# Layer 1's inverse one product later, and three edits around the first values and the last queries

## The chip, the cores and the metric

The kernel runs on one core of a Trainium2 chip. The metric is device time in microseconds from start to end of the program, as a median of several runs. A run with the hardware profiler gives one execution instruction by instruction; its times are counted from the span's start.

## The reference

Input x has 8 elements of 512 channels by 1024 tokens (32 x 32), fp32. Layer 0 is multi-head attention with 8 heads, layer 1 attention with one head:

```python
# layer 0, per element; x as tokens x channels
xn = layer_norm(x) * gamma + beta            # over channels
q, k, v = (xn @ W.T + b for ...)             # 8 heads of 64
out = softmax(q k^T / 8) v @ Wo.T + bo + x
# layer 1, per element; x as channels x tokens
h = group_norm(x, 32 groups) * gamma + beta
q, k, v = wq h + bq, wk h + bk, wv h + bv
out = x + wp (softmax(q^T k / sqrt(512)) v) + bp
```

## The kernel before

**Products by seven.** Every large matrix product is split into 2 x 2 blocks and computed with seven block products instead of eight, after Strassen and Winograd. `STEPS` lists the seven: which left block or sum (S1 to S4), which right block or difference (T1 to T4), and which of three accumulators x, z, y in PSUM it goes to. The first, second and fourth open x, z and y; the others add onto them. Steps here are counted first to seventh; the code's index is one less. A `Product` is one unit, that is half of the output rows; there are two units to a projection. `multiply` issues a step's matmuls, `tick` pops a number of small jobs (`pieces`) from the deque `side`, and `leave` takes out what the step has completed:

- after the first step ScalarE copies x to a buffer u(0, 0), after the third to u(0, 1), and after the fourth it copies y to u(1, 1);
- after the second VectorE adds z to u(0, 0), after the fifth x to u(1, 1), after the sixth y to u(0, 1) (L386);
- after the seventh ScalarE copies x out as block (1, 0).

So the sixth step, which adds onto y, needs the copy of y done, and the seventh needs the addition of x done. `lead` issues the first half of a step's contraction early.

**Stages of an element.** Layer 0's keys and queries (`project`, from the second element on `project_deep`, which splits the blocks once more and needs "deep" sums of the normed input, L574 to L579), values (`project_v`), the heads' scores and values in pairs, the output projection (`project_out`); then layer 1's group norm (`GroupNorm`), queries, scores (`Whole.scores`), values `vm`, and `Whole.values`, the product of probabilities and values: units `o_units`, accumulators x_o, z_o, y_o, matmuls at L506. All but the last element compute layer 1's queries with `project_mixed`; the last one uses `project` with leads, between the two halves of its group norm.

**Layer 1's inverse.** The softmax's denominators are summed over keys on VectorE and GpSimd, folded by a chain of DMAs into a tile of 128 x 512 (L861, L865), and `Whole.inverse` makes reciprocals of them in three parts: `invert` on VectorE (transpose L869, reduction, reciprocal L1121), `copies` (eight small ScalarE copies, L1455), and `rows` (a VectorE transpose that expands them to rden, L855). The order around it is

```python
            o_units[1].step(2)
            inverse = whole.inverse()
            next(inverse)              # invert
            next(check, None)
            o_units[0].step(1)
            next(inverse)              # copies
            o_units[0].step(1)
            next(inverse)              # rows
```

after which both units' finished blocks are scaled by rden (L1491), have the residual added (L1493, a GpSimd DMA that accumulates) and go out (L1496). Then unit 0 does its fifth to seventh steps and unit 1 its third to seventh, with two ticks each; the deep sums of the next element's normed input are queued after unit 1's third.

**What sets the order.** TensorE, ScalarE, VectorE and GpSimd run in the order in which the program is written (`tc.manual_schedule(engines=ORDERED)`); SP, which issues most loads and stores, is not in that list and is ordered by the framework. Jobs in `side` (the next layer norm's pieces, deep sums, operand differences) fall where ticks fall. A layer norm puts itself back at the second place of `side` after each piece. Semaphores come from the framework, by tiles.

**PSUM.** Three wide tiles of 128 x 1024 (`wide_psum`) and two of 128 x 512 (`bank`). In `banks_of`, y is a bank of its own for each unit; an accumulator named in `own` is a wide tile of its own for each unit (of which 512 columns are used), and any other is one wide tile shared, half and half. The default is `own="x"`.

**Group norm.** `GroupNorm.part` (L1087 to L1117) takes a slice of the chunks: aggregate the statistics, two small products with `grp` in a tile from `self.bank` (pm), the root, and then the normed blocks `gn`, of which some go to ScalarE (L1114) and the others to VectorE (L1116). The last element norms its chunks in two halves, one chunk of each pair at a time, with pm in a wide tile.

Of the kernel before, what the change touches and what calls it, by code (L numbers as in the profile page):

```python
# [71 lines left out]
def fast_path(ctx: ExitStack, tc: tile.TileContext, x: bass.AP, vecs: dict, weights: dict, out: bass.AP,  # L72
# [32 lines left out]
    def big_tile(name):  # L105
        return big.tile([P, S], F32, tag="b", name=name)
# [10 lines left out]
    def block(name):  # L117

        return big_tile(name).rearrange("p (a t) -> p a t", a=2)

    def wide(blk):
        return blk.rearrange("p a t -> p (a t)")
# [56 lines left out]
    ua = const.tile([P, NC], F32, tag="ua", name="ua")  # L179
# [167 lines left out]
    def later(*work):  # L347
        side.extend(work)
# [128 lines left out]
    def channel_part(r):  # L477

        def part(dst, a, b, opens, ks=(0, 1)):
            for k in ks:  # L480
                nc.tensor.matmul(dst, a[:, k, ts(r, P)], b[:, k, :], start=(opens and k == 0), stop=(k == 1),  # L481
                                 skip_group_check=True)
        return part
# [29 lines left out]
    def project(tag, w, bias, h, apart=False, own="x"):  # L513

        res, shared = {}, None if apart else {}

        def unit(r):
            def dest(i, k):
                if (i, k) not in res:
                    res[i, k] = block(f"{tag}_{i}{k}")  # L520
                return res[i, k][:, r, :]

            def shift(u, ps, which, add=None):
                nc.scalar.activation(u, ps, AF.Identity, bias=bias(2 * which[0] + r))

            return Product(f"{tag}_{r}", w, h, channel_part(r), shift, dest,
                           banks_of(tag, r, shared, own))
        return [unit(r) for r in range(2)], res
# [287 lines left out]
    def project_v(tag, w, h, apart=False):  # L816


        res, shared = {}, None if apart else {}

        def unit(r):
            def dest(i, k):
                if (i, k) not in res:
                    res[i, k] = big_tile(f"{tag}_{i}{k}")
                return res[i, k][:, ts(r, HB)]

            return Product(f"{tag}_{r}", w, h, token_part(r), plain_shift, dest, banks_of(tag, r, shared))
        return [unit(r) for r in range(2)], res
# [6 lines left out]
    def operands(h):  # L835

        return {"tag": h["tag"], **{f"{j + 1}{k + 1}": h[j, k] for j in range(2) for k in range(2) if (j, k) in h}}

    def add_operand(b, n):
        b[n] = block(f"{n}_{b['tag']}")  # L840
        l, r = {"T1": ("12", "11"), "T2": ("22", "T1"), "T3": ("22", "12"), "T4": ("21", "T2")}[n]
        nc.vector.tensor_sub(wide(b[n]), wide(b[l]), wide(b[r]))

    def add_operands(b):
        later(*(lambda n=n: add_operand(b, n) for n in ("T1", "T2", "T3", "T4") if n not in b))


    def compact(t, ps):
# [213 lines left out]
    class GroupNorm:  # L1062
# [10 lines left out]
        def part(self, chunks):  # L1073

            own = list(range(NC // 2))[chunks]
            n = 2 * len(own)
            name = f"{self.b}_{own[0]}"

            def of(t):
                return t.rearrange("p (j a) -> p a j", j=2)[:, chunks, :]  # L1080

            def wide_of(t):
                return t[:, :n].rearrange("p (a j) -> p a j", j=2)

            for a in own:
                for j in range(2):
                    c = 2 * j + a  # L1087
                    nc.vector.bn_aggr(self.mv[:, c, :], self.stats[:, c, :, :].rearrange("p a s -> p (a s)"))
            mu, var = (of(self.mv[:, :, i]) for i in range(2))
            mean, dev, sc, sh = (of(t) for t in (self.mean, self.dev, self.sc, self.sh))  # L1090
            yield
            ps = self.bank(f"pm_{name}")
            pm = wide_of(ps)
            nc.tensor.matmul(pm, grp, mu, start=True, stop=True)
            nc.vector.tensor_copy(mean, pm)
            nc.vector.tensor_sub(dev, mu, mean)
            nc.vector.tensor_mul(dev, dev, dev)
            nc.vector.tensor_add(dev, dev, var)
            yield
            pv = wide_of(ps[:, 2 * NC :])  # L1100
            nc.tensor.matmul(pv, grp, dev, start=True, stop=True)
            inverse_root(sc, pv, "gsc")()
            nc.vector.tensor_mul(sc, sc, of(vt[:, VECS.index("g1"), :]))
            nc.vector.tensor_mul(sh, mean, sc)
            nc.vector.tensor_sub(sh, of(vt[:, VECS.index("be1"), :]), sh)
            for j, k in ((0, 0), (1, 0), (0, 1), (1, 1)):
                if (j, k) not in self.h:
                    self.h[j, k] = block(f"gn_{self.b}_{j}{k}")
                for a in own:
                    c = 2 * j + a  # L1110
                    m, d = self.sc[:, c : c + 1], self.sh[:, c : c + 1]
                    h, x = self.h[j, k][:, a, :], self.xt[j, k][:, a, :]
                    if a == own[0] and k == 0:
                        nc.scalar.activation(h, x, AF.Identity, bias=d, scale=m)  # L1114
                    else:
                        nc.vector.tensor_scalar(h, x, m, d, ALU.mult, ALU.add)  # L1116
            yield  # L1117
# [426 lines left out]
    def bias_of(n):  # L1544
        return lambda oc: vec(n, oc)

    with tc.manual_schedule(engines=ORDERED):
# [51 lines left out]
        units, kt = project("k0", wk_now, bias_of("bk0"), hb)  # L1599
# [5 lines left out]
        units, qt = project("q0", wq_now, bias_of("bq0"), hb)  # L1605
# [7 lines left out]
        save_deep_later("q", wq_now)  # L1613
        save_deep_later("a", wa, (1, 2))
        units, vts = project_v("v0", wv_now, hb)
        for u in units:
            u.pieces = 2
            u.rest()
        for b in range(B):
            more = b + 1 < B  # L1620
# [43 lines left out]
            o_units, x1 = project_out(b, wo_now, ob, stats)  # L1664
# [8 lines left out]
            wa_now = load_w("a", b)  # L1673
            if more:
                wa_deep = load_deep("a", b, (1, 2))
            gn = GroupNorm(b, x1, stats)
# [27 lines left out]
            h1b = operands(h1)  # L1704
# [3 lines left out]
            if more:  # L1708
                def vn_put_away():
                    for ik, t in vn.items():  # L1710
                        vn_away[ik] = put_away(t, f"v_away_{b + 1}_{ik[0]}{ik[1]}")
                    if ln:
                        ln.sums()

                vn_away = {}
                spare = list(x1)
                whole = Whole(b, {}, h1b, x1_away)

                def ready(t):
                    whole.q["11"] = t  # L1720
                    whole.query_prime("11")

                qa, closing = project_mixed(f"qa{b}", wa_now, wa_deep, lambda oc: ua[:, oc : oc + 1], h1b, primes,
                                            lambda: n_units[1].step(1), vn_put_away,
                                            lambda: residual(*spare.pop(0)), ready)
                whole.q["12"] = qa[1, 0]
                whole.deep_query("12")
                closing(whole.q)
            else:
                a_units, qa = project(f"qa{b}", wa_now, lambda oc: ua[:, oc : oc + 1], h1b, own="")  # L1730
                h1b["T1"] = t1
                leads = [(u, i) for i in (0, 1, 3) for u in a_units]
                until(lambda: not side)
                for n, _ in enumerate(gn.part(slice(1, 2))):
                    for u, i in ((leads[:3], leads[3:4], leads[4:])[n]):
                        u.lead(i)
                nc.vector.tensor_sub(t1[:, 1, :], h1[0, 1][:, 1, :], h1[0, 0][:, 1, :])
                add_operands(h1b)
                a_units[0].step(2)
                a_units[1].step(2)  # L1740
                away = list(x1)
                for n, (_, name) in enumerate(SINGLES):
                    deep_operands_later(h1b, h1_deep, [name])
                    later(*(lambda ik=ik: residual(*ik) for ik in away[n : n + 1]))
                for u in a_units:
                    u.pieces = 2
                a_units[0].rest()
                whole = Whole(b, qa, h1b, x1_away)
                whole.deep_query("11")
                a_units[1].step(5)  # L1750
                whole.deep_query("12")
# [16 lines left out]
            o_units = whole.values(vm)  # L1768
# [7 lines left out]
                ln.queue()  # L1776
            o_units[1].step(2)
            inverse = whole.inverse()
            next(inverse)
            next(check, None)  # L1780
            o_units[0].step(1)
            next(inverse)
            o_units[0].step(1)
            next(inverse)
            for u in o_units:
                u.hold = False
# [413 lines left out]
```

## Time and profile before

| | |
|---|---|
| median of 3 runs | 2809.73 us (2807.9 to 2809.82) |
| the profiled execution | 2808.93 us; its span 2807.1 us |
| TensorE busy | 2789.8 us of the span (99%) |
| VectorE, ScalarE, GpSimd busy | 2095.0, 1248.4, 527.6 us |
| granted TensorE clock | 0.999 |
| first x_o to first x_k, element 0 to 6 | 49.07, 49.35, 48.34, 49.86, 48.35, 49.50, 48.06 us |

A timeline line gives start and duration in us, engine, line of the program, operation, output and inputs with shapes, and the number of instructions merged; a bracket gives the idle time before it and what ended it. A line of the waits gives the total in us, how often, and the longest.

### The profile page before, as it was taken

The numbers are of one execution on the slowest core, as the hardware profiler recorded it, in microseconds if no ns is written. First come the engines' busy times: TensorE is split into PE (matmuls) and PEld (weight loads), VectorE is DVE, ScalarE is ACT, GpSimd is POOL, SyncE is SP. The second block draws the span as 40 slices with busy tenths as digits, with TensorE's granted clock in tenths as the row PEclk, the third lists the DMA queues.
The fourth block names the chain that finished last, engine by engine and source line by source line (L and its number), as shares of the span: only waits on it lengthen the run. The fifth ranks groups of instructions, "written<-read, shape, count | busy, mean of one in ns | idle before, by whom it ended". The sixth has DMA issues, their size and how long they took to land.

```text
span 2807.1 us, 31693 instructions
## 1 busy us (share of the span) xinstructions
PE 2789.8 (99%) x10959; PEld 1624.5 (58%) x10959; DVE 2095.0 (75%) x2978; ACT 1248.4 (44%) x2114; POOL 527.6 (19%) x724
## 2 busy tenths in 40 slices
PE   9999999999999999999999999999999999999999
PEld 4535756358563685536854467644676347663375
DVE  6677877778777777777867777678867778657775
ACT  4463425724257242662436533365334733336341
POOL 2031022210222102220122211222112210122001
PEclk9999999999999999999999999999999999999999
DMA  8245367353763547536474464744448433373224
GB/s 314 95 96 126 109 163 189 69 149 111 170 160 70 166 107 184 126 78 190 108 177 109 88 186 107 200 79 119 149 112 207 100 94 117 82 195 64 65 79 99
DMA packets 141018, 365.56 MB, mean 130 GB/s; under 512 B 19776, under 2 KB 24176, under 8 KB 140848
## 3 DMA queue, kind: packets, MB, share of 16 engines
q0 software_dynamic: 58992, 144.22, 27.7%
q1 hardware_dynamic: 81760, 219.19, 22.6%
q8 instruction: 89, 1.46, 0.2%
q14 instruction: 81, 0.66, 0.1%
q10 hardware_dynamic: 96, 0.02, 0.0%
HBM read 198.21 MB, written 63.44 MB: 93 GB/s over the span
## 4 chain that ended last, share of the span: by engine, by line
PE 93%; DMA 3%; DVE 2%; issue 1%; POOL 0%; ACT 0%; SPq 0%; POOLq 0%; DVEq 0%; ACTq 0%
PE s L1154 16%; PE acc L1172 16%; PE s L1320 7%; PE x_o L506 6%; PE x_v L490 4%; PE x_out L481 4%; PE x_vm L490 3%; PE y_s L1320 3%; PE y_o L506 3%; PE y_v L490 2%; PE s L1355 2%; PE y_out L481 2%; PE x_k L604 2%; PE x_q L604 2%; PE c_qa L698 2%; PE y_vm L490 1%
## 5 line engine op out<-in xcount | busy, mean ns | idle before, releaser
L1163 DVE TENSOR_TENSOR sum<-sum,p 128x1024 f32<-128x1024 f32 x384 | 470.3, 1225 | 39.4 <-DVE sum L1161 0.5
L1157 ACT ACTIVATE p<-s 128x1024 f32<-128x1024 f32 (+1 forms) x608 | 478.8, 984 | 15.1 <-PE s L1154 15.1
L1172 PE MATMUL acc<-p,v_again 128*64 128x512 f32 x1792 | 390.9, 594 | 0.0
L1172 PEld LDWEIGHTS acc<-p,v_again 128*64 128x64 f32 x1792 | 126.1, 137 | 261.3 <-issue 236.7
L861 POOL DMA_DIRECT2D fold<-sum x312 | 207.7, 759 | 302.8 <-DMA sum<-sum 176.7
L1154 PE MATMUL s<-q,k 64*128 64x512 f32 x1152 | 252.1, 592 | 0.0
L1154 PE MATMUL s<-q_lower,k_lower 64*128 64x512 f32 x896 | 196.1, 592 | 0.0
L1161 DVE TENSOR_TENSOR sum<-p,p 128x1024 f32<-128x1024 f32 x64 | 78.2, 1221 | 154.5 <-ACT p L1157 154.5
L1154 PEld LDWEIGHTS s<-q,k 64*128 64x128 f32 x1152 | 109.7, 186 | 138.2 <-issue 84.9
L865 POOL DMA_DIRECT2D sum<-sum x78 | 63.5, 814 | 456.6 <-DVE sum L1163 232.5
L1154 PEld LDWEIGHTS s<-q_lower,k_lower 64*128 64x128 f32 x896 | 85.4, 186 | 110.5 <-issue 68.5
L1176 ACT COPY o<-acc 128x512 f32<-128x512 f32 x63 | 36.9, 586 | 221.7 <-PE acc L1172 221.5
L1360 DVE TENSOR_TENSOR p<-p,p 128x1024 f32<-128x1024 f32 x96 | 114.0, 1214 | 6.3 <-ACT p L511 6.3
L506 PE MATMUL x_o<-T_p,S_vm 128*128 128x512 f32 x256 | 115.2, 592 | 0.0
L511 ACT COPY u(0, 0)_v<-x_v 128x512 f32<-128x512 f32 x16 | 9.4, 586 | 186.5 <-PE x_v L490 186.5
L1416 POOL DMA_DIRECT2D sum<-p x32 | 28.0, 934 | 334.2 <-ACT p L1308 240.8
L490 PE MATMUL x_vm<-w_m,T_gn 128*128 128x256 f32 x384 | 90.7, 379 | 0.0
L481 PE MATMUL x_out<-T_o,w_o 128*128 128x512 f32 x192 | 89.2, 594 | 0.0
L506 PEld LDWEIGHTS x_o<-T_p,S_vm 128*128 128x128 f32 x256 | 48.6, 190 | 60.7 <-issue 60.7
L1218 ACT COPY rr<-r 32x16 f32<-32x16 f32 x256 | 53.5, 209 | 62.0 <-DVE r L1121 58.6
L490 PE MATMUL x_v<-w_v,T_h 128*128 128x256 f32 x336 | 80.0, 381 | 0.0
L490 PEld LDWEIGHTS x_vm<-w_m,T_gn 128*128 128x128 f32 x384 | 72.9, 190 | 10.0
(621 smaller groups left out, 5456.1 us busy)
## 6 DMA issues: line engine op xcount, KB each, us to landing
sum<-sum POOLq DMA_DIRECT2D x78, 256.0 KB, 3.4
fold<-sum POOLq DMA_DIRECT2D x312, 64.0 KB, 2.3
x<-in_x_dram SPq DMA_DIRECT2D x32, 512.0 KB, 4.7
xr<-in_x_dram SPq DMA_DIRECT2D x64, 256.0 KB, 4.9
x_away<-x SPq DMA_DIRECT2D x32, 512.0 KB, 3.3
sum<-p POOLq DMA_DIRECT2D x32, 512.0 KB, 5.9
v_away<-v SPq DMA_DIRECT2D x28, 512.0 KB
v_again<-v_away SPq DMA_DIRECT2D x28, 512.0 KB, 7.3
```

Of the source, the lines that this page charges most:

```text
L481: nc.tensor.matmul(dst, a[:, k, ts(r, P)], b[:, k, :], start=(opens and k == 0), stop=(k == 1), skip_group_check=True)
L490: nc.tensor.matmul(dst[:, ts(m, CB)], b[:, k, ts(2 * r + m, P)], a[:, k, :], start=(opens and m == 0 and k == 0), stop=(k == 1), skip_grou ...
L506: nc.tensor.matmul(dst, a[:, m, ts(r, P)], b[m // 2][:, m % 2, :], start=(opens and m == 0), stop=(m == NM // 2 - 1), skip_group_check=True)
L604: nc.tensor.matmul(dst[:, ts(s, CB)], a[s], b[s], start=(opens and s == 0), stop=True, skip_group_check=True)
L861: nc.gpsimd.dma_start(out=f[ts(q + i, BL), :], in_=t[ts(n, BL), ts(i, HB)], accum_op=ALU.add if n else ALU.bypass)
L1154: nc.tensor.matmul(parts[i], self.k[m // 4][r, ts(m % 4, P)], self.q[r, :], start=True, stop=True)
L1157: nc.scalar.activation(dst, src, AF.Exp, scale=1.0 / float(D) ** 0.5)
L1161: nc.vector.tensor_add(self.sum, self.p[0], p)
L1163: nc.vector.tensor_add(self.sum, self.sum, p)
L1172: nc.tensor.matmul(acc[i * D : (i + 1) * D, :], value_of(self.vt, m, self.c * P + i * D, D), self.p[m][:, ts(i, HB)], start=(m == 0), stop ...
L1320: nc.tensor.matmul(dst[:, ts(c, CB)], x[0][:, ts(c, P)], a[0], start=(opens and c == 0), stop=True, skip_group_check=True)
L1360: nc.vector.tensor_add(wide(t), wide(t), wide(x))
```

## The change

Four edits, and one that lets a queued operand be made earlier:

- In all elements but the last, unit 0's third step comes ahead of `invert`, its fourth ahead of `copies`, and unit 1's third ahead of `rows`. Unit 1's third step thus comes before unit 0's fifth, with one tick in place of two.
- In the last element's queries each unit has an x tile of its own, all three wide tiles are opened ahead of the second half of the group norm, and that half's pm is a bank.
- There, T2 is queued first and an empty job after it, so that T3 is made two ticks later than before, behind unit 0's first addition. `add_operands` skips what is there already.
- In a group norm of one chunk (the last element's halves) ScalarE takes the second token half instead of the first, and VectorE the first. With two chunks nothing changes.
- In the first element's values, unit 0's first step has no tick.

```diff
     def add_operands(b):
-        later(*(lambda n=n: add_operand(b, n) for n in ("T1", "T2", "T3", "T4") if n not in b))
+        later(*(lambda n=n: n in b or add_operand(b, n) for n in ("T1", "T2", "T3", "T4") if n not in b))
...
-                    if a == own[0] and k == 0:
+                    if a == own[0] and k == len(own) % 2:
...
         units, vts = project_v("v0", wv_now, hb)
+        units[0].pieces = 0
+        units[0].step(1)
         for u in units:
...
-                a_units, qa = project(f"qa{b}", wa_now, lambda oc: ua[:, oc : oc + 1], h1b, own="")
+                a_units, qa = project(f"qa{b}", wa_now, lambda oc: ua[:, oc : oc + 1], h1b)
+                for u, to in ((0, "x"), (0, "z"), (1, "x")):
+                    a_units[u].open(to, True)
+                gn.bank = bank
...
                 nc.vector.tensor_sub(t1[:, 1, :], h1[0, 1][:, 1, :], h1[0, 0][:, 1, :])
+                later(lambda: add_operand(h1b, "T2"), nothing)
                 add_operands(h1b)
...
             inverse = whole.inverse()
+            if more:
+                o_units[0].step(1)
             next(inverse)
             next(check, None)
             o_units[0].step(1)
             next(inverse)
-            o_units[0].step(1)
+            o_units[0 if not more else 1].step(1)
             next(inverse)
```

## The prediction

> **What bounds the kernel now.** I read the page's head first, then TensorE's waits, then the timeline around each wait.
>
> ```profile
> span 2807.1 us, 31693 instructions
> ...
> PE 2789.8 (99%) x10959; PEld 1624.5 (58%) x10959; DVE 2095.0 (75%) x2978; ACT 1248.4 (44%) x2114; POOL 527.6 (19%) x724
> ...
> PE 93%; DMA 3%; DVE 2%; issue 1%; POOL 0%; ACT 0%; SPq 0%; POOLq 0%; DVEq 0%; ACTq 0%
> ```
>
> TensorE is idle for 17.3 of 2807.1 us, and the change takes no matmul away. So the whole stake is a part of those 17.3 us, and what matters is which holes the edits reach. The list of waits on TensorE names them (total, times, longest):
>
> ```profile
> PE y_o L506 <- ACT u(1, 1)_o L511: 1.9, 3, 0.9
> PE x_o L506 <- DVE u(1, 1)_o L386: 1.3, 4, 0.3
> PE x_qa L481 <- ACT gn L1114: 0.8, 1, 0.8
> PE x_qa L481 <- ACT qa L524: 0.8, 1, 0.8
> PE z_qa L481 <- DVE qa L386: 0.8, 1, 0.8
> PE x_v L490 <- ACT u(0, 0)_v L511: 0.4, 1, 0.4
> ```
>
> The rest is the start of the kernel and its tail, which the change doesn't touch. A wait costs more than its entry, since the refill behind it is not in the list; so I measure holes by start times. The timeline of element 3 (the fourth) shows the repeated one, TensorE first, then ScalarE, then VectorE:
>
> ```profile
> 1420.41 3.60 PE L506 MATMUL x_o<-T_p,S_vm 128*128 128x512 f32 x8
> 1424.94 3.70 PE L506 MATMUL y_o<-p,S_vm 128*128 128x512 f32 x8 [0.93 <-ACT u(1, 1)_o L511]
> 1428.96 3.70 PE L506 MATMUL x_o<-T_p,vm 128*128 128x512 f32 x8 [0.32 <-DVE u(1, 1)_o L386]
> ...
> 1422.58 1.70 ACT L1455 COPY rr<-r 32x16 f32<-32x16 f32 x8 [4.76 <-DVE r L1121]
> 1424.30 0.59 ACT L511 COPY u(1, 1)_o<-y_o 128x512 f32<-128x512 f32 x1
> ...
> 1420.06 0.71 DVE L869 STREAM_TRANSPOSE fold1t<-fold 128x512 f32<-128x512 f32 x1 [5.55 <-DMA fold<-sum]
> 1428.26 0.65 DVE L386 TENSOR_TENSOR u(1, 1)_o<-u(1, 1)_o,x_o 128x512 f32<-128x512 f32 x1
> ```
>
> The folded sums land late, VectorE inverts them late, ScalarE's eight small copies of the inverse wait for that, and the copy that frees bank y (its product ended near 1420.4) stands behind them in the queue. Unit 0's sixth product needs that bank; its seventh then waits for VectorE's sum, which is behind the inverse as well.
>
> [...] the 0.59 us copy starts only at 1424.30, when the small copies end. [...] The trace does show such waits (x_qa at 2676.84 below): this program waits by tile, so a tile per unit removes them. [...]
>
> **Layer 1's inverse, elements 0 to 6.** A product of a unit is 8 records at 0.429 us, 3.433 us by start times. From the first x_o to the first x_k there are 14, which is 48.06 us. Element 6 takes 48.06 (2426.57 to 2474.63). The others take 49.07, 49.35, 48.34, 49.86, 48.35, 49.50. Their losses are 1.01 + 1.29 + 0.28 + 1.80 + 0.29 + 1.44 = **6.11 us**. Element 6 has no layer norm to prepare, and its fold lands early.
>
> The edit moves unit 0's third product ahead of the inversion, the fourth ahead of the small copies, and unit 1's third ahead of the row expansion. Let F be the time from the start of unit 0's third product to VectorE's fold transpose: 5.73, 6.00, 5.00, 6.51, 5.02, 6.17 us in elements 0 to 5. It ends a chain of GpSimd's DMAs that no moved instruction feeds, so I keep it.
> - Bank y: product four ends 6.9 us after that start. Its copy is now ahead of the small copies and is done by 7.7; the sixth product starts at 4 x 3.433 = 13.7. This wait goes.
> - The sum before the seventh product. VectorE from F: inversion 2.52, small copies on ScalarE 1.74, rden 1.26, two scalings 1.22, expansion of mu 1.16. One tick more has gone by, so a centring (L967, 1.17) now stands there too, and the mean's folding (2.15) has moved ahead of the inversion, into VectorE's wait. Then the sum, 0.65. That is F + 9.7 = 16.2 at worst, against 5 x 3.433 = 17.17. Cover left: 0.9 us in element 3, 2.4 in elements 2 and 4.
> - What is late next: unit 1's third product is no longer followed by two ticks. The deep operands of the next keys therefore start one product later and have one piece fewer behind them at the hand-over. In element 3, K is x_k's start, 1449.67. VectorE's last scaling starts at K + 0.81 in both. Before, three pieces followed until 22_deep was complete at 1453.48 = K + 3.81; now 21's first piece (L574, 0.70) joins them: K + 4.51. x_k reads it at 1454.41 = K + 4.74. With 0.05 for the semaphore (sum ends 1428.91, TensorE starts 1428.96) **0.2 us** of cover is left. If it is gone, each 0.1 late costs 0.1 plus a refill of 0.1, six times over.
> - Queues moved past: GpSimd's additions (L1493) and SP's output stores follow the scalings, which stay at F + 6.8 in elements 0 to 5. In element 6 they come one product, 3.4 us, later; SP's w_k_deep loads behind them were issued by 2457.1 and take 7.5 us to land, so they arrive by 2468 for an x_k at 2474.6. The next layer norm's x landed tens of us before (issued by 1383 for a use at 1429).
>
> I take the full 6.11. If the seventh product still waits and 22_deep is late, some 0.3 each, it is 6.11 - 6 x 0.6 = 2.5. It can't exceed 6.11.
>
> **First element's values.** z_v starts at 99.55 and y_v at 103.69: 4.14 us for two products of 1.727, **0.69 us** lost. Unit 0's first copy stands behind a squaring (100.28 to 101.33) which a tick put there. Without that tick it follows q's copy (99.70 to 100.28) and ends near 100.9, ahead of the 101.28 at which x_v can start. The squaring moves into the next tick. Bounds 0 and 0.69; I take 0.69. No instruction is added; two pieces pass to the pairs' ticks.
>
> **Last element's queries.**
>
> ```profile
> 2663.16 1.12 PE L481 MATMUL x_qa<-gn,w_a 128*128 128x512 f32 x2 [0.78 <-ACT gn L1114]
> 2666.94 1.12 PE L481 MATMUL z_qa<-gn,w_a 128*128 128x512 f32 x2 [0.76 <-DVE qa L386]
> ...
> 2674.18 1.88 PE L481 MATMUL x_qa<-T_gn,w_a 128*128 128x512 f32 x4
> 2676.84 1.98 PE L481 MATMUL x_qa<-T_gn,w_a 128*128 128x512 f32 x4 [0.78 <-ACT qa L524]
> ```
>
> - First normed block: VectorE writes one in 0.54 (L1116), ScalarE in 0.82 here. x_qa can start at 2662.29 + 0.54 + 0.05 = 2662.88 instead of 2663.16.
> - T1's second half (2663.21) and T2 (2663.93, next start 2665.07) stay; T2's other operand, now from ScalarE, is ready at 2663.81. Without T3 in between, the sum that reads z runs from 2665.07 to 2665.75, not 2666.21 to 2666.89. z is still one tile, so unit 1's z starts at 2665.80 instead of 2666.94: **1.14 us**, the 0.28 within it. T3 then ends at 2666.9, for a use at 2669.4.
> - The x tile: unit 1's third product follows unit 0's seventh at once, 1.72 instead of 2.66 us later: **0.94 us**.
> - Given back: a residual's pair of activations (1.3 us) falls between two of unit 1's copies, as it does in unit 0 now: 0.03 to 0.1. The statistics' products move to a bank, since three tiles hold all the wide space. The last lead, y_qa of unit 1, gets that bank after VectorE's read at 2661.28, where it would start anyway (2661.27), and has until 2662.88.
>
> Sum **2.05 us**. Bounds: 0.9 (the x tile alone) and 2.9 (the list's three waits with their refills, of which the first can't vanish wholly).
>
> **Sum.** 6.11 + 0.69 + 2.05 = 8.85 us. The profiled execution took 2808.93 us (span 2807.1, the rest around it): 2800.1. The median of the runs is 0.8 above it, so 2809.73 - 8.85 = **2800.9 us**.
>
> **Rivals.**
> 1. *Part of it is eaten*: the 0.2 us at 22_deep or the 0.9 us ahead of the seventh product doesn't hold. For it: both covers are small and F moves by 1.5 us between elements. Against: each is worked from rows of the same stretch. Gain 4 to 7, about 2804.
> 2. *The change doesn't do what it says*: F grows, since GpSimd's fold transfers drift and meet others, or SP's free order puts another wait in; the holes reappear a product later. Against: F is at most 6.5 and would have to reach some 10 for bank y's user to wait as now. Gain 0 to 3, about 2808.
> 3. *Slower*: the next keys' weights come late. SP's order isn't written out, and its w_k and w_k_deep loads stand behind stores that wait for the scalings. If x_k then waits in all seven elements, it decides for slower by 0.2% from (5.6 + 8.85) / 7 = 2.1 us each; at 2.5 us it is 2800.9 + 17.5 = 2818. For it: stores and loads share a queue. Against: landing by about 1442.6 for 1449.7 in element 3, 7 us before its use, 5 after the gain; no wait on a DMA is listed for TensorE in any element's body.
>
> **How the numbers follow.** About 0.2% (5.6 us) is what a measurement of this kernel can tell from no change. As worked out (2799.3 to 2803, scatter of the runs included): 0.70. Rival 1: 0.15, half of it beyond 5.6. Rival 2: 0.07. Rival 3: 0.08. Faster 0.70 + 0.07 = 0.77, same 0.08 + 0.07 = 0.15, slower 0.08. The range is 2799.3 (the bounds' 9.7 us, less likely in full, and a 0.7 us lower run) to 2805.8, which takes in most of rival 1: about 0.8.
>
> **What would show it.** Right: no y_o or x_o wait at L506; ScalarE's u(1, 1)_o copy ahead of the eight L1455 copies; 48.1 us from the first x_o to the first x_k in every element; in the first values z_v to y_v 3.45; in the last element, z_qa near 1.1 earlier against the first x_qa lead, and no x_qa wait on qa. Wrong: an x_k wait on 22_deep (L578 or L579), an x_o wait on VectorE in element 3, or any TensorE wait on w_k.

## The result, and the profile after

| | before | after |
|---|---|---|
| median of 7 runs each | 2809.73 us (2807.9 to 2810.03) | 2800.16 us (2798.97 to 2800.33) |
| span of the profiled execution | 2807.1 us | 2797.2 us |
| first x_o to first x_k, elements 0 to 6 | 49.07, 49.35, 48.34, 49.86, 48.35, 49.50, 48.06 us | 48.06 to 48.07 us in all |
| F (third step's start to the fold transpose), elements 0 to 5 | 5.73, 6.00, 5.00, 6.51, 5.02, 6.17 us | 5.82, 7.10, 4.69, 6.66, 4.64, 6.28 us |
| first values, z_v to y_v | 4.14 us | 3.46 us |
| last element, first x_qa lead to the first score | 28.37 us | 26.34 us |

The ratio of the times is 0.9967, with a 95% interval of 0.9955 to 0.9979. Here are the head of the changed kernel's page, with busy time, share and count, and its chain that ended last:

```profile
span 2797.2 us, 31704 instructions
...
PE 2786.4 (100%) x10959; PEld 1625.5 (58%) x10959; DVE 2095.1 (75%) x2978; ACT 1248.2 (45%) x2114; POOL 527.6 (19%) x724
...
PE 99%; DMA 0%; DVE 0%; ACT 0%; issue 0%; SPq 0%; DVEq 0%
```

The matmuls are as many as before, and the other engines are as busy as before. TensorE's idle time fell from 17.3 to 10.8 us, and the chain that ended last now stays on TensorE almost throughout. These are TensorE's longest waits in the changed kernel (total, times, longest):

```profile
PE pst_k L301 <- DMA w_k<-in_L_conv_wk_dram: 1.8, 1, 1.8
PE ps_first L1550 <- DVE checks L142: 1.3, 1, 1.3
PE pm L1094 <- DVE mv L1088: 0.6, 1, 0.6
PE x_qa L481 <- DVE gn L1116: 0.4, 1, 0.4
```

Of the six waits that the prediction showed, one is still in this list: x_qa's on the normed block, cut from 0.8 to 0.4 us. Of z_qa's wait on the sum, 0.14 us are left in the trace, too little for the list. The first two lines belong to the start of the kernel (both end before 20 us), and the third was there before, with the same 0.6 us. The same stretch of element 3 in the changed kernel's timeline, TensorE first, then ScalarE, then VectorE:

```profile
1416.36 7.03 PE L506 MATMUL x_o<-T_p,S_vm 128*128 128x512 f32 x16
1423.22 3.60 PE L506 MATMUL y_o<-p,S_vm 128*128 128x512 f32 x8
1426.66 3.60 PE L506 MATMUL x_o<-T_p,vm 128*128 128x512 f32 x8
...
1416.61 0.58 ACT L511 COPY u(1, 1)_o<-y_o 128x512 f32<-128x512 f32 x1 [2.85 <-PE y_o L506]
1418.67 1.70 ACT L1455 COPY rr<-r 32x16 f32<-32x16 f32 x8 [1.47 <-DVE r L1121]
...
1416.15 0.71 DVE L869 STREAM_TRANSPOSE fold1t<-fold 128x512 f32<-128x512 f32 x1 [3.75 <-DMA fold<-sum]
1424.16 1.23 DVE L967 TENSOR_TENSOR x<-x,mu 128x1024 f32<-128x1024 f32 x1
1425.30 0.68 DVE L386 TENSOR_TENSOR u(1, 1)_o<-u(1, 1)_o,x_o 128x512 f32<-128x512 f32 x1
```

The copy of y now stands ahead of the eight small copies and waits for nothing but its own product. VectorE still waits 3.75 us for the fold, and the fold is as late as before: F is 6.66 us here, and was 6.51. But TensorE has one more product to do meanwhile: the 16 records at 1416.36 are unit 1's third and unit 0's fifth. The sum ends at 1425.98, 0.68 us ahead of the seventh product.

The last element's timeline in the changed kernel, TensorE only:

```profile
2655.33 1.12 PE L481 MATMUL x_qa<-gn,w_a 128*128 128x512 f32 x2 [0.43 <-DVE gn L1116]
...
2658.31 1.13 PE L481 MATMUL z_qa<-gn,w_a 128*128 128x512 f32 x2
...
2665.55 3.60 PE L481 MATMUL x_qa<-T_gn,w_a 128*128 128x512 f32 x8
```

Unit 1's z product starts 2.98 us after the x_qa, where it was 3.78, and both units' third products run as one group of eight records, where the second had to wait.

The spans differ by 9.9 us: 6.1 in the inverses, 0.7 in the first values and 2.0 in the last queries, which is 8.8. Another 0.8 lies ahead of the first x_v, in code that the change doesn't touch: x_v starts at 97.82 us before and at 97.01 after, and it lies between 97.0 and 98.4 in all profiles of this study. The remaining 0.3 is in the tail with its output transfers.

### The profile page after: what moved, and what is told of

It is laid out like the page before. It is cut to its first block, busy times and chain, and to the rows that moved or that the text cites. A ratio compares the mean times of both kernels' runs of the same rounds, so it can differ in the third digit from the quotient of the medians.

```text
span 2797.2 us, 31704 instructions
## 1 busy us (share of the span) xinstructions
PE 2786.4 (100%) x10959; PEld 1625.5 (58%) x10959; DVE 2095.1 (75%) x2978; ACT 1248.2 (45%) x2114; POOL 527.6 (19%) x724
## 4 chain that ended last, share of the span: by engine, by line
PE 99%; DMA 0%; DVE 0%; ACT 0%; issue 0%; SPq 0%; DVEq 0%
PE s L1154 16%; PE acc L1172 16%; PE x_o L506 8%; PE s L1320 7%; PE x_v L490 4%; PE x_vm L490 4%; PE y_o L506 4%; PE x_out L481 4%; PE y_s L1320 3%; PE y_v L490 2%; PE y_vm L490 2%; PE s L1355 2%; PE y_out L481 2%; PE z_o L506 2%; PE x_q L604 2%; PE x_k L604 2%
## 5 line engine op out<-in xcount | busy, mean ns | idle before, releaser
L506 PE MATMUL x_o<-T_p,S_vm 128*128 128x512 f32 x256 | 114.0, 592 | 0.0
L506 PEld LDWEIGHTS x_o<-T_p,S_vm 128*128 128x128 f32 x256 | 48.6, 190 | 60.7 <-issue 60.5
```

What stands on the lines that cost most here:

```text
L506: nc.tensor.matmul(dst, a[:, m, ts(r, P)], b[m // 2][:, m % 2, :], start=(opens and m == 0), stop=(m == NM // 2 - 1), skip_group_check=True)
```

## The experiments

My theory was that ScalarE's queue behind the late fold makes the holes of the inverse, that one more product on TensorE covers it, and that the waits by tile and the order of VectorE's sums make those of the last queries. The rivals were that only part of a gain is kept, that the holes come back later, and that the cover at 22_deep is nearly used up.

### One part at a time

The kernel before with the inverse's edit alone:

```diff
             inverse = whole.inverse()
+            if more:
+                o_units[0].step(1)
             next(inverse)
             next(check, None)
             o_units[0].step(1)
             next(inverse)
-            o_units[0].step(1)
+            o_units[0 if not more else 1].step(1)
             next(inverse)
```

> The inverse's edit alone. Theory (the queue order on ScalarE and VectorE made the holes): first x_o to first x_k is 48.06 in all seven elements, no TensorE wait at L506, 6.1 us below the kernel before (ratio 0.9978). Rival (the gain of the whole change is mostly elsewhere, or the start of the kernel): less than 4 us.

Measured: 2802.43 us against 2809.2 for the kernel before on the same chip, ratio 0.9976 (0.9967 to 0.9985), so 6.8 us. All elements take 48.06 to 48.07 us, and the last queries stay at 28.39. The inverse's edit acts alone and in full.

The kernel before with the last element's edits alone:

```diff
-        later(*(lambda n=n: add_operand(b, n) for n in ("T1", "T2", "T3", "T4") if n not in b))
+        later(*(lambda n=n: n in b or add_operand(b, n) for n in ("T1", "T2", "T3", "T4") if n not in b))
...
-                    if a == own[0] and k == 0:
+                    if a == own[0] and k == len(own) % 2:
...
-                a_units, qa = project(f"qa{b}", wa_now, lambda oc: ua[:, oc : oc + 1], h1b, own="")
+                a_units, qa = project(f"qa{b}", wa_now, lambda oc: ua[:, oc : oc + 1], h1b)
+                for u, to in ((0, "x"), (0, "z"), (1, "x")):
+                    a_units[u].open(to, True)
+                gn.bank = bank
...
+                later(lambda: add_operand(h1b, "T2"), nothing)
                 add_operands(h1b)
```

> The last element's three edits alone (a tile x for each unit, T3 later, first normed block on VectorE). Theory: from the first x_qa lead to the first score 26.3 us instead of 28.37, so 2.05 us below before; the elements keep their L506 waits (losses of some 6 us). Rival: below 1 us, since a later stage takes it back.

Measured: 2807.4 us, ratio 0.9993 (0.9984 to 1.0001). The time alone can't tell this from no change. The trace can: the lead-to-score stretch takes 26.35 us instead of 28.37. It also shows something about the inverse, whose order is here that of the kernel before: its elements lose 7.06 us in this execution, where they lost 6.1 in the one that I had worked from. The fold came 6.83 us after the third product in element 1, instead of 6.00, which is most of the difference.

The kernel before with the first values' edit alone:

```diff
         units, vts = project_v("v0", wv_now, hb)
+        units[0].pieces = 0
+        units[0].step(1)
         for u in units:
```

> The missing tick in the first element's values alone. Theory: z_v to y_v 3.46 us instead of 4.14; 0.7 us in all, less than a measurement tells. Rival: the squaring that moves into the next tick delays a later copy, and the 0.7 come back before the first score s.

Measured: 2809.02 us, ratio 0.9998 (0.999 to 1.0007). z_v to y_v takes 3.45 us instead of 4.14, and from x_v to the first score it is 25.47 instead of 26.16, so the 0.69 us aren't given back there. The inverse's losses are 7.19 us in this execution. The three medians together differ from before by 6.8 + 1.8 + 0.2 = 8.8 us, against 9.6 for the whole change; with the intervals above, that is the same.

### Is the late fold the root?

The kernel before, in its old order, with the halving ahead of layer 1's fold left out. This leaves part of the sum out of the denominators (half of the rows that should be added), and with it transfers of the chain on which VectorE waits:

```diff
         def fold(self):
             self.f = half_tile(f"fold1_{self.b}")
-            for hf in range(NH):
-                halve(self.total[hf])
             for hf in range(NH):
                 fold(self.f, 2 * hf, self.total[hf])
```

> The kernel before with layer 1's fold made shorter: the DMA additions of the upper 64 rows (halve) are left out there, so layer 1's denominators miss half of their rows; all else is as before. Theory (the holes come from the late fold, which the queues pass on): VectorE's fold transpose comes some 3 us after unit 0's third product instead of 5 to 6.5, and all seven elements take 48.06 with the order unchanged: 6.1 us below before. Rival (the order itself costs, whenever the fold lands): the holes of 0.3 to 1.8 us stay.

Measured: 2802.58 us, ratio 0.9976 (0.9966 to 0.9986), with 48.06 to 48.07 us in every element although no product was moved. F is 0.9 to 2.0 us; I had expected some 3. The fold's tile in this kernel, with VectorE's idle time ahead of it and how often:

```profile
  DMA fold<-sum: 2.9, 4
```

The kernel before has 28.9 us in 7 such waits. So the fold's lateness is the root, and moving products (6.8 us) gains what an early fold gains (6.6).

### Would ScalarE's order have been enough?

The kernel before with the small copies put behind unit 0's fourth product, and unit 1's third left where it was:

```diff
             inverse = whole.inverse()
+            if more:
+                o_units[0].step(1)
             next(inverse)
             next(check, None)
             o_units[0].step(1)
             next(inverse)
-            o_units[0].step(1)
+            if not more:
+                o_units[0].step(1)
             next(inverse)
```

> The kernel before with one thing moved: unit 0's fourth product ahead of the small copies; unit 1's third product stays where it was, and the inversion stays ahead of unit 0's third. Bank y's copy is then ahead of the small copies. Theory: no y_o wait, but the sum ahead of the seventh product ends at about F + 8.5 against 13.7, so x_o waits of about 0.5, 0.8, 0, 1.3, 0 and 1.0 us with their refills in elements 0 to 5: some 4 of the 6.11 us stay. Rival (the queue order on ScalarE is all there is): every element takes 48.06.

Measured: 2811.81 us in a single run, beside 2809.7. The elements take 48.92, 49.93, 48.20, 51.91, 48.13, 49.98 and 48.06 us, a loss of 8.7, where I had expected about 4. The wait for bank y is gone; TensorE's waits in this kernel name what stands in its place:

```profile
PE x_o L506 <- DVE u(1, 1)_o L386: 5.7, 4, 1.9
```

Without unit 1's product in between, the seventh comes 4 x 3.433 = 13.7 us after the third, but VectorE's sum ends F + 8.85 after it, 15.7 in element 3. I had put it at F + 8.5, since I forgot the mean's folding (2.15 us at L869 to L940, where I had counted 1.74 for the small copies), which here, as in the kernel before, stands between the inversion and rden.

So the order on ScalarE gains nothing by itself, and the comparison with the kernel before says more than that: the wait for bank y never set the loss. Four profiles have the whole fold and lack the additional product: before, the last queries alone, the first values alone, and this one. In each of their elements 0 to 5 the loss is F - 4.73 us to within 0.02, with y's copy behind the small copies or ahead of them; elements 3 and 4 of this kernel are the exceptions. (In element 4, F - 4.73 is below zero and 0.06 us are lost; on element 3 see below.) VectorE takes 8.85 us from the fold transpose to the end of the sum in all of them (9.00 in that element 4), as in element 3 here:

```profile
1421.09 0.71 DVE L869 STREAM_TRANSPOSE fold1t<-fold 128x512 f32<-128x512 f32 x1 [5.91 <-DMA fold<-sum]
1429.29 0.65 DVE L386 TENSOR_TENSOR u(1, 1)_o<-u(1, 1)_o,x_o 128x512 f32<-128x512 f32 x1
```

The seventh product starts 0.05 us after that sum. In the kernel before, the sixth product's wait for bank y was a part of the same hole, taken one product early. What gains is the 3.4 us of work that TensorE does in the meantime. Whether y's copy has to be moved at all was not run. In the three profiles with the old order it ends F + 4.83 us after the third product starts, 11.3 in element 3 before; with one product more the sixth would start at 13.7, so by this estimate the additional product alone would have covered that wait as well.

In element 3, 1.70 us more were lost than F - 4.73. Its timeline, TensorE only:

```profile
1429.99 5.40 PE L506 MATMUL x_o<-T_p,vm 128*128 128x512 f32 x8 [1.88 <-DVE u(1, 1)_o L386]
1435.23 3.60 PE L506 MATMUL x_o<-T_p,S_vm 128*128 128x512 f32 x8
```

The eight records behind the hole take 5.24 us by start times, not 3.43. Stretches of the same kernel, two in element 3 and, beside them, one with the gap of element 5, say why (length; busy us of TensorE, weight load, VectorE, ScalarE and GpSimd, each with its count; granted clock; DMA share; GB/s):

```profile
1427.47:1430.89 3.42, 1.54 (x4) 0.49 (x3) 3.39 (x6) 0.00 (x0) 1.82 (x2) 1.00 0.41 48
1430.89:1434.30 3.41, 3.41 (x5) 1.35 (x4) 3.38 (x5) 2.11 (x2) 0.87 (x1) 0.50 0.96 159
...
2113.55:2116.96 3.41, 1.76 (x5) 0.66 (x4) 3.38 (x5) 0.00 (x0) 1.82 (x2) 1.00 0.44 65
```

The granted clock is 0.50 for 3.41 us behind the hole, which is 1.7 us of time. TensorE's gap between products was 2.0 us here (5.47 from start to start of two products of 3.43), and the half clock began 0.9 us after its end. Elements 1 and 5 had gaps of 1.8 us of the same kind, and no slower products behind them (3.54 and 3.53 us by start times, with 0.1 of refill). In the stretch ahead of the half clock TensorE was busy for 1.54 of 3.42 us, and in that of element 5, at a clock of 1.00, for 1.76 of 3.41. What sets the one gap apart from the other two was not shown.

### The last element, edit by edit

From here on the base is the kernel after. First, both units share one x tile again, and the second half's statistics are back in a wide tile:

```diff
-                a_units, qa = project(f"qa{b}", wa_now, lambda oc: ua[:, oc : oc + 1], h1b)
-                for u, to in ((0, "x"), (0, "z"), (1, "x")):
-                    a_units[u].open(to, True)
-                gn.bank = bank
+                a_units, qa = project(f"qa{b}", wa_now, lambda oc: ua[:, oc : oc + 1], h1b, own="")
```

> The changed kernel with the x tile shared again by both units of the last queries (and the statistics in a wide tile). Theory: the 0.94 us wait of unit 1's third product on the copy of qa is back, so first lead to first score 27.3 us instead of 26.34. Rival (the tile is not what is waited for): 26.3.

Measured: 2801.21 us in a single run; lead to score takes 27.39 us, 1.05 more than after. In its timeline the wait of unit 1's third product is back, 0.94 us by start times, to which 0.1 us of refill comes (the four records behind the wait take 1.99 us, the four ahead of it 1.88):

```profile
2669.34 1.99 PE L481 MATMUL x_qa<-T_gn,w_a 128*128 128x512 f32 x4 [0.78 <-ACT qa L524]
```

Next, T3 made at its old place, ahead of the first addition:

```diff
-                later(lambda: add_operand(h1b, "T2"), nothing)
```

> The changed kernel with T3 queued at once again. Theory: unit 1's z waits for the sum behind T3, 1.14 us later, so first lead to first score 27.5 us. Rival: the x tile already took this wait, 26.3.

Measured: 2802.42 us in a single run; lead to score takes 27.48 us, 1.14 more than after. Unit 1's z product waits:

```profile
2660.86 1.12 PE L481 MATMUL z_qa<-gn,w_a 128*128 128x512 f32 x2 [1.28 <-DVE qa L386]
```

Third, the first normed block written by ScalarE again:

```diff
-                    if a == own[0] and k == len(own) % 2:
+                    if a == own[0] and k == 0:
```

> The changed kernel with the first normed block on ScalarE again. Theory: x_qa starts 0.28 us later, but unit 1's z is set by VectorE's T1, T2 and sum, so first lead to first score stays within 0.05 of 26.34: this edit is hidden by the wait behind it. Rival: 26.6, the 0.28 is on the path.

Measured: 2801.56 us in a single run; lead to score takes 26.46 us, 0.12 more than after. The wait is 0.27 us longer than after's 0.43:

```profile
2657.06 1.13 PE L481 MATMUL x_qa<-gn,w_a 128*128 128x512 f32 x2 [0.70 <-ACT gn L1114]
```

Of the 0.27 us at this place, 0.15 are made up at unit 1's z, which then waits less; 0.12 are kept. I had expected it to be hidden almost wholly.

### How much cover is left at 22_deep?

The kernel after, with one product more of unit 1 issued ahead of the queuing of the deep sums:

```diff
-            o_units[1].step(1)
+            o_units[1].step(2 if more else 1)
```

> The changed kernel with the next keys' deep sums queued behind unit 1's fifth product instead of its fourth, so two pieces more are left at the hand-over. Theory (0.2 us of cover in the changed kernel): the deep sum of 22 is complete at about x_k's start + 5.3 against a need at 4.7, so x_k waits 0.6 us with a refill of 0.1 in elements 0 to 5, 4 us in all over the changed kernel; element 6, which has no layer norm between, doesn't wait. If only the slice that is read counts, some 0.2 each and 1 us in all. Rival (cover is larger than worked out): no wait.

Measured: 2809.26 us, ratio to before 0.9999 (0.999 to 1.0007), so nearly the whole gain is lost. The stretch from the first x_k to the first x_q takes 22.93 us instead of 21.56 in each of the elements 0 to 5, and is unchanged in element 6. Six times 1.37 is 8.2 us, twice what I had expected; a wait of 0.7 us for a w_q_deep load comes once beside it. In element 3 of this kernel, TensorE, then VectorE:

```profile
1456.69 0.70 PE L604 MATMUL x_k<-22_deep_h,w_k_deep 128*128 128x256 f32 x2 [1.10 <-DVE 22_deep_h L578]
...
1455.02 1.28 DVE L386 TENSOR_TENSOR k<-u(0, 0)_k,z_k 128x512 f32<-128x512 f32 x2
1456.21 0.42 DVE L578 TENSOR_TENSOR 22_deep_h<-22_deep_h,x 128x256 f32<-128x256 f32 x1
1456.67 0.43 DVE L579 TENSOR_TENSOR 22_deep_h<-x,22_deep_h 128x256 f32<-128x256 f32 x1
```

Two things are to be seen here. First, 22_deep's last piece has fallen behind two additions of k (1.19 us from their start to that of L578), because they are issued before the deep sums are emptied from the queue; I had left them out, and they make the wait larger than I thought. Second, x_k starts at 1456.69, 0.06 us after L578 ends (1456.63) and well before L579 ends (1457.10). It needs only the part that L578 writes. So the waits of this program aren't by whole tiles everywhere, as I had put it above: here the instruction that writes the slice counted, while x_qa's wait on the other unit's half (0.78 us, gone with a tile for each unit) went by the tile. So in the kernel after, where L578 ends at K + 4.09 with x_k due at K + 4.74, the cover is 0.6 us, not the 0.2 that I had worked out from L579.

### What is still to be had

The kernel after, with unit 1's z product later, so that it no longer waits for the sum that reads z:

```diff
                 a_units[0].step(2)
-                a_units[1].step(2)
+                a_units[1].step(1)
+                a_units[0].step(1)
+                a_units[1].step(1)
```

> The changed kernel with unit 0's third product of the last queries put between unit 1's first and second. Theory: unit 1's z no longer waits for the sum (0.3 us with the refill), first lead to first score 25.95 to 26.05 instead of 26.34. Rival: T2 is not ready in time and the wait only moves, 26.3.

Measured: 2799.62 us in a single run; lead to score takes 25.75 us, 0.59 less than after, where I had expected 0.29 to 0.39. The z product now follows its neighbours without a gap; gaps of less than 0.1 us between the products behind it are gone as well.

The same, and in addition one more product of the output projection ahead of the first statistics of the group norm:

```diff
-                for _ in gn.part(slice(0, 1)):
-                    o_units[1].step(1)
+                for n, _ in enumerate(gn.part(slice(0, 1))):
+                    o_units[1].step(2 if n == 0 else 1)
...
-                a_units[1].step(2)
+                a_units[1].step(1)
+                a_units[0].step(1)
+                a_units[1].step(1)
```

> The last one's edit, and unit 1's fourth output product put ahead of the first statistics product of the last group norm. Theory: the wait of pm (0.56 us) goes, but the first half's norm comes 1.2 us later and pushes VectorE's chain to the second half's statistics, so x_qa's wait grows by 0.4 to 0.9 and little is won over the last kernel: within 0.5 us of it. Rival: VectorE has room, 0.6 us less.

Measured: 2799.01 us (2798.86 to 2800.41), ratio to before 0.9963 (0.9949 to 0.9977). The first half's wait at pm is gone, but the second half's product with the statistics now waits, as TensorE's timeline of this kernel shows:

```profile
2652.00 0.38 PE L1094 MATMUL pm<-mv,grp 128*128 128x2 f32 x2 [0.31 <-DVE mv L1088]
```

I had expected it at x_qa, whose wait stays as it was (0.44). From the first x_out to the first score it takes 51.30 us, against 51.42 without this second edit and 52.00 in the kernel after. It has the lowest median of the study, but its interval overlaps that of the change, and 0.7 us aren't told apart by timing.

## Why the prediction was right

The forecast of 2800.9 us stands against 2800.16. Point by point:

- **The inverse, 6.11 us.** Right in place and in the cure: 48.06 us in every element, no wait at L506, and the short fold shows that the fold's lateness is the root. Of the two waits in it, the prediction put ScalarE's queue first; but only VectorE's sum, which it named second, set the loss, and the copies behind the fourth product show this. The size, and with it "it can't exceed 6.11", came from one execution, in which the fold of element 1 was early. In the two other executions with the old order (the last queries alone, the first values alone) the losses were 7.1 and 7.2 us, of which F in element 1 (6.83 and 6.94 instead of 6.00) makes 0.8 and 0.9, and the inverse's edit alone gained 6.8 by the medians. Put at 6.8, it would have brought the forecast to within 0.1 us; that the rest is scatter is argued, not shown.
- **"F is at most 6.5", and with it the 0.9 us of cover in element 3.** The term was too narrow. F was 7.10 in element 1 after, and the sum there ended 0.23 us ahead of the seventh product, 0.18 with the semaphore's 0.05. The sum's end, F + 9.83 in element 3, was right at F + 9.7. The cover held, but it is a fifth of what the prediction named, and it lies in another element. In a later profile (one x tile shared again) F was 7.19 there, and the sum ended 0.13 us ahead of the seventh product: the full gain in element 1 hangs on the fold not coming much later than in these profiles.
- **22_deep, 0.2 us.** Too small by its own step: the piece that x_k waits for is L578, not L579, and the cover is 0.6 us. Of the two covers, the one that I had put at 0.9 us is the thin one.
- **The first values, 0.69 us.** 0.68 measured, and kept up to the scores.
- **The last queries, 2.05 us.** 2.03 measured; 1.14 for T3's place and 1.05 for the x tile, of which the latter was put at 0.94. The two add up to 2.19 and the first normed block brings 0.12 more, so the parts overlap: what one is worth depends on the others being there. That block's share was said to lie within T3's 1.14; what it is worth on top is 0.12.
- **Slower by late weights.** Excluded: no wait for w_k or w_k_deep in any element's body after the change. **Doing nothing**: excluded by the same 48.06 us.

## What to carry to other kernels

When a saturated engine waits behind a chain that can't be made faster, look for a product that doesn't depend on the chain, and put it between; reordering the queue that holds a release back may only turn the wait into the next one, as the copies behind the fourth product did. Of several waits in one hole, ask which one ends last: it alone sets the loss. Work out each cover from the instruction that writes the slice that is read (here L578, which ended 0.06 us ahead of x_k's start), and name all that is popped ahead of it. And take a chain of transfers from several executions before its lateness is used as a bound: here F moved by up to 1.3 us in the same element (3.86 to 5.16 in element 2, in two profiles with the same order at that place).

## What the runs showed of the hardware that I had not expected

In the kernel with the small copies behind the fourth product, a gap of 2.0 us on TensorE was followed once by 3.41 us at a granted clock of 0.50, which cost 1.7 us, nearly as much as the gap; two gaps of 1.8 us in the same execution were not. And in the kernel with the deep sums queued later, a matmul was released 0.06 us after the writer of the slice that it reads had ended, while the next instruction on VectorE still wrote another slice of that tile for 0.41 us more.
